# Listed rows turned by VectorE in 32 by 32 blocks, counts from two products, the last block added half by half: one AdaLN block with a mixture of experts on Trainium2

## The chip, the cores and the metric

The kernel runs on one core of a Trainium2 chip. The metric is the device time of one execution in microseconds. Nine runs of the kernel before have a median of 868.95 us (864.46 to 876.58).

## What is computed

One transformer block over `x` of 8 sequences by 512 tokens by 256 features, all in float32. The first half is a layer norm with a modulation, a causal linear attention of 16 heads and an output projection, added to `x`. The second half is a layer norm with a modulation and a mixture of 8 experts. Its core, from the reference:

```
probs = jax.nn.softmax(xf @ router_w.T, axis=-1)
topv, topi = jax.lax.top_k(probs, 2)
topv = topv / (topv.sum(axis=-1, keepdims=True) + 1e-09)
cw = (jax.nn.one_hot(topi, e, dtype=xf.dtype) * topv[..., None]).sum(axis=1)
h = jax.nn.gelu(jnp.einsum('td,edh->teh', xf, w1), approximate=False)
y = jnp.einsum('teh,ehd->ted', h, w2)
out = jnp.einsum('te,ted->td', cw, y)
```

`w1` is 8 by 256 by 1024 and `w2` 8 by 1024 by 256: 1 MB each for one expert. The kernel computes only the two experts that a token is routed to.

## The kernel before, in words

**Routing.** The eight sequences are worked on one after the other, in chunks of 128 tokens. `rows_of` makes one row of 521 floats for each token (256 normed features, the token's number, 8 weights, 256 gate values). `route` (L884) ranks the 8 experts for each token and counts, for each token and expert, how many tokens came before it. That count comes from products into the PSUM tile `at_ps` (L918 to L930): one with the strictly triangular matrix `earlier`, and one with `ones` for each of the four chunks, over all later chunks. With the count, POOL scatters each row twice into the DRAM array `slots` (L963), which has a list for each expert.

**Blocks.** Full units of a list are taken as soon as they are there (`plan`), the rest at the end (`plan_rest`). A block is a pair (256 rows) or a single (128 rows) of one expert. By `TAKE` (L34) there are 9 singles and 10 pairs during the sequences; 17 pairs and 4 singles follow from `plan_rest`, and four more singles stand in a branch at the end that is taken only if a list needs it. That makes 27 pairs and 13 singles outside the branch.

**One block.** `fetch` (L1206) has SP load the expert's `w1` (L1216), its `w2` (L1221) and the rows (L1227, tile `r`), in this order, three buffers of each; which expert and which rows is read from SBUF into a register first. `turn_rows` (L1241) turns the rows: PE transposes of 128 by 128 into PSUM (`x_ps`, L1253), an ACT copy to SBUF (`xT`, L1255). Then `experts` (L1342) alternates first products (`h_ps`, from `w1` and `xT`), ACT's gelu (`g`) and second products (`y_ps`, in `second`, L1282). `finish` (L1295) multiplies `y_ps` by weight and gate on DVE into `y`, and POOL adds each half of 128 rows to the sums with an indirect DMA (L1321): to `acc` in DRAM, and for the last five blocks to the output itself, once `acc` has been copied there (L1306).

**Order.** Nothing is issued as the code is read. All work goes into a plan (`Plan`), which simulates the engines with written-in durations and then issues each engine's instructions in the order found. On each engine this order is fixed: PE waits at a product whose weights are late, and SP waits at a load whose buffer isn't free, with all later loads behind it. A buffer of `w1` becomes free with the last first product of the block three before; one of `w2` with its last second product.

All engine instructions go through a helper and so show line L220; tile names tell them apart.

Of the kernel before, what the change touches and what calls it, by code (L numbers as in the profile page):

```python
# [19 lines left out]
HEADS = 16  # L20
HD = 16
HALF = HD // 2
PAIR = 2 * HD
GH = P // HD
LN_EPS = 1e-5
# [313 lines left out]
def kernel(  # L339
# [57 lines left out]

    SYNC = mybir.DependencyInfo(mybir.DependencyClass.Sync, mybir.DependencyReason.DATA)
    scattered = []
    gathered = []  # L400
    added = []
    copied = []
# [481 lines left out]
    def route(q):  # L884
# [30 lines left out]
        is_in = small([P, NC, E], "is_in")  # L915
        first = small([P, NC, 2, E], "first")
        dve(V.tensor_single_scalar, is_in, rank, 2.0, op=ALU.is_lt)
        at_ps = early_bank(f"at_ps_{b}")  # L918
        with L.group("PE", 1.05):
            product(  # L920
                at_ps[:, : NC * E], earlier, is_in.rearrange("p c e -> p (c e)"),
                start=True, stop=False, skip_group_check=True,
            )
            for c in range(NC):

                product(
                    at_ps[:, (c + 1) * E : (NC + 1) * E].rearrange("p (c e) -> p c e", e=E),
                    ones, is_in[:, c, :].unsqueeze(1).to_broadcast([P, NC - c, E]),
                    start=False, stop=(c == NC - 1), skip_group_check=True,
                )  # L930
        dve(V.tensor_reduce, red, pr, us=0.18, axis=AX.X, op=ALU.add)
        dve(V.tensor_scalar_add, red, red, 1e-9 * LARGE)
        dve(V.reciprocal, red, red)
# [23 lines left out]
        dve(V.tensor_reduce, where, first, us=0.21, axis=AX.X, op=ALU.add)  # L957
        dve(V.tensor_copy, slot, where)
        dve(V.tensor_add, count, count, at_ps[:, NC * E : (NC + 1) * E])
        q.scatters = []  # L960

        def scatter(c, j):
            s = nc.gpsimd.indirect_dma_start(  # L963
                out=slots, out_offset=IndirectOffsetOnAxis(ap=slot.now()[:, c, j : j + 1], axis=0),
                in_=row.now()[:, c, :], in_offset=None,
                bounds_check=NONE - 1, oob_is_err=False,
            )
            apart(s, scattered + cleared, "a slot is of one pair of token and expert")
            apart(s, gathered, "blocks that are read are full by then")
            scattered.append(s)  # L970

        L.level += LEVEL["scatter"]
        for c in range(NC):
            for j in range(2):
                q.scatters.append(
                    L.do(
                        "POOL", 1.29, lambda c=c, j=j: scatter(c, j), r=[slot, row], landing=2.0,
                        mb=0.27,
                    )
                )  # L980
                q.scatters[-1].indirect = True


    def spans(small, n, tag):
# [221 lines left out]
    def fetch(block):  # L1206
        n, nt = block.n, block.nt
        L.level = TOP
        w1_sb = L.tile(wpool, [P, KD, H], "w1", f"w1_{n}", 3)
        w2_sb = L.tile(wpool, [P, NH, D], "w2", f"w2_{n}", 3)  # L1210
        r = L.tile(pb, [P, 2, ROW], "r", f"r_{n}", 3)
        reg = {}

        def weights1():
            reg["e"] = nc.sync.value_load(block.expert_i.now(), min_val=0, max_val=E - 1)
            nc.sync.dma_start(  # L1216
                out=w1_sb.now(), in_=w1[ds(reg["e"], 1)].rearrange("o (k p) h -> p (o k) h", p=P)
            )

        def weights2():  # L1220
            nc.sync.dma_start(  # L1221
                out=w2_sb.now(), in_=w2[ds(reg["e"], 1)].rearrange("o (n p) d -> p (o n) d", p=P)
            )

        def rows():
            at = nc.sync.value_load(block.slot.now(), min_val=0, max_val=NONE)
            got = nc.sync.dma_start(  # L1227
                out=r.now()[:, :nt, :],
                in_=slots[ds(at, nt * P), :].rearrange("(t p) w -> p t w", p=P),
            )  # L1230
            needed = [g for w in block.seen for g in w.given]
            behind(got, needed, "the rows of a block come before it")
            apart(got, [s for s in scattered if s not in needed], "those are of later blocks")
            gathered.append(got)

        L.do("SP", 0.6, weights1, r=[block.expert_i], w=[w1_sb], landing=2.0, mb=1.0)
        L.do("SP", 0.4, weights2, r=[block.expert_i], w=[w2_sb], landing=2.0, mb=1.0)
        L.do("SP", 0.6, rows, r=[block.slot], w=[r], after=block.seen, landing=2.0, mb=0.26 * nt)
        return block, w1_sb, w2_sb, r

    def turn_rows(fetched):  # L1241

        block, w1_sb, w2_sb, r = fetched
        n, nt = block.n, block.nt
        L.level = 1000 + X.k - 1.5
        rest = block.held is not None
        x_ps = late_bank(f"x_ps_{n}") if rest else early_bank(f"x_ps_{n}")
        w = nt * P
        xT = L.tile(pb, [P, KD, 2 * P], "xT", f"xT_{n}", 2)
        with L.group("PE", 0.11 * 2 * nt, hold=[xT]):  # L1250
            for k in range(KD):
                for t in range(nt):
                    turn(x_ps[:, k * w + t * P : k * w + (t + 1) * P], r[:, t, ts(k, P)])  # L1253
        L.level = TOP
        copy(xT[:, :, :w], x_ps[:, : KD * w].rearrange("p (k s) -> p k s", k=KD))  # L1255
        cw = L.tile(pb, [P, 2, 1], "cw", f"cw_{n}", 3)
        cwe = L.tile(pb, [P, 2, E], "cwe", f"cwe_{n}", 3)
        dve(
            V.tensor_mul, cwe[:, :nt], r[:, :nt, CW:GATE],
            block.is_of.unsqueeze(1).to_broadcast([P, nt, E]),  # L1260
        )
        dve(V.tensor_reduce, cw[:, :nt], cwe[:, :nt], us=0.17, axis=AX.X, op=ALU.add)
        to = L.tile(pb, [P, 2], "to", f"to_{n}", 3, I32)
        dve(V.tensor_copy, to[:, :nt], r[:, :nt, TID].bitcast(I32))
        if rest:

            empty = L.tile(pb, [P, 2], "empty", f"empty_{n}", 3, I32)
            instead = L.tile(pb, [P, 2], "instead", f"instead_{n}", 3, I32)
            dve(
                V.tensor_tensor, empty[:, :nt], block.held[:, block.i, :].to_broadcast([P, nt]),  # L1270
                place[:, :nt], op=ALU.is_le,
            )
            fits = block.at_end and nt == 2
            dve(V.tensor_copy, instead[:, :nt], (place if fits else beyond)[:, :nt])
            L.call(
                "DVE", 0.17,
                lambda o, m, d: V.copy_predicated(out=o, mask=m, data=d),
                to[:, :nt], empty[:, :nt], instead[:, :nt], 
            )
        return block, w1_sb, w2_sb, xT, cw, to, r  # L1280

    def second(y_ps, w2_sb, nt, group, n_groups, each, g, level):  # L1282

        L.level = level
        with L.group("PE", 0.433 * each * nt):
            for t in range(nt):
                for i in range(each):
                    product(
                        y_ps[:, ts(t, D)], g[:, i * nt * P + t * P : i * nt * P + (t + 1) * P],
                        w2_sb[:, each * group + i, :],  # L1290
                        start=(group == 0 and i == 0 and t == 0),
                        stop=(group == n_groups - 1 and i == each - 1), skip_group_check=True,
                    )

    def finish(block, cw, to, r, y_ps):  # L1295
        n, nt = block.n, block.nt
        L.level = TOP
        y = L.tile(pb, [P, 2, D], "y", f"y_{n}", 2)
        for t in range(nt):
            dve(  # L1300
                V.scalar_tensor_tensor, y[:, t, :].of(t), y_ps[:, ts(t, D)], cw[:, t, :],
                r[:, t, GATE:], us=0.48, op0=ALU.mult, op1=ALU.mult,
            )
        if block.at_end and X.copies is None:
            def give(b):
# [7 lines left out]
            ]  # L1313
        after = X.adds[-2:] + X.stores[-1:] + (X.copies or [])

        def add():
            halves = []
            for t in range(nt):
                if t:
                    nc.gpsimd.memset(between, 0.0)  # L1320
                s = nc.gpsimd.indirect_dma_start(  # L1321
# [4 lines left out]
                    oob_is_err=nt == 2 or not block.at_end,  # L1326
                )
                apart(s, halves, "a token comes to an expert once")
                behind(s, added[-1:], "one addition to a token after the other")
                if block.at_end:  # L1330
                    behind(s, copied, "and after the sums so far")
                halves.append(s)
            added.extend(halves)

        X.adds.append(
            L.do("POOL", 1.85 * nt, add, r=[to, y], after=after, landing=2.0, mb=0.13 * nt)
        )
        X.adds[-1].indirect = True

    X.stores = []  # L1340

# [58 lines left out]
    for b in range(B):  # L1400
# [20 lines left out]
        route(q)  # L1421
        if TAKE[b][0]:
            L.level = 4 * b + 3 + LEVEL["plan"]
            blocks = plan(b, q.scatters)
            experts(blocks)
    L.level = 4 * B
    blocks, others, more_i = plan_rest(q.scatters)

    def all_of(blocks):
        experts(blocks)  # L1430
        second(*X.pending)
        finish(*X.ending)
        X.pending = X.ending = None

    def give_out():
# [66 lines left out]
```

## Time and profile before

| | |
|---|---|
| median of nine runs | 868.95 us |
| the profiled execution, its own time | 870.08 us |
| its span, first to last instruction | 868.4 us |
| PE busy | 808.3 us (93%) |
| PE weight loads busy | 666.7 us (77%) |
| DVE / ACT / POOL busy | 381.1 / 284.1 / 319.5 us |
| moved by DMA | 154.27 MB in 95167 packets |
| share of the 16 DMA engines, SP's queue / POOL's queue | 44.8% / 12.6% |
| mean granted PE clock | 0.968 |

PE is the busiest engine. The span falls in three parts: up to about 425 us attention and routing with the nine singles in between, then a mixture until about 500 us, then expert blocks alone. "Busy" is time in which an instruction of the engine ran; the idle time of an engine that isn't the bottleneck costs nothing. A "packet" is one contiguous piece that one of the 16 DMA engines moves.

### The profile page before, as it was taken

The page shows a single profiled execution, that of the slowest core. Times are in us where ns is not written, and L with a number is a line of the kernel's source. Part 1 is how long each engine was busy: PE and PEld are TensorE (multiplying, and loading weights), DVE is VectorE, ACT ScalarE, POOL GpSimd, SP SyncE. Part 2 cuts the span into 40 slices and gives each one's busy share as a digit, 9 for nine tenths or more (in the row PEclk, how much of TensorE's full clock was granted, in tenths as well). Part 3 has the DMA queues.
Part 4 walks back from the last instruction along what each step waited for, and adds up shares of the span by engine and source line. Part 5 has one row for each costly group of instructions (what it writes and reads, how often), then busy time and mean ns, then how long its engine had stood idle before and what let it go on. Part 6 is the DMA issues. An engine that isn't in the chain of part 4 may idle for free. (4 is left out here: it accounts for less than half of the span.)

```text
span 868.4 us, 15967 instructions
## 1 busy us (share of the span) xinstructions
PE 808.3 (93%) x5998; PEld 666.7 (77%) x5998; DVE 381.1 (44%) x1290; ACT 284.1 (33%) x617; POOL 319.5 (37%) x477
## 2 busy tenths in 40 slices
PE   5899886998979979899999899999999999999995
PEld 3566665766857867678888688888898989889885
DVE  4889776588777848767527010111111111111000
ACT  3555342443625536354222112222122221222120
POOL 5733544426463453543515612212122112212122
PEclk9999988899999989999999899999999999999999
DMA  7412343853535252624957967667686867858942
GB/s 221 122 29 68 98 151 138 297 140 117 161 131 159 79 186 88 217 70 153 286 181 232 279 189 213 218 185 225 168 258 228 247 177 236 263 176 259 348 89 26
DMA packets 95167, 154.27 MB, mean 178 GB/s; under 512 B 6632, under 2 KB 69736, under 8 KB 94960
## 3 DMA queue, kind: packets, MB, share of 16 engines
q1 hardware_dynamic: 79680, 125.22, 44.8%
q0 software_dynamic: 15408, 28.00, 12.6%
q8 instruction: 49, 0.80, 0.4%
q14 instruction: 30, 0.25, 0.1%
HBM read 120.19 MB, written 37.20 MB: 181 GB/s over the span
## 5 line engine op out<-in xcount | busy, mean ns | idle before, releaser
L220 PE MATMUL y_ps<-w,g 128*128 128x256 f32 x1072 | 257.4, 383 | 7.0 <-issue 7.0
L220 PE MATMUL h_ps<-xT,w 128*128 128x256 f32 (+1 forms) x1280 | 258.2, 352 | 0.2 <-PE x_ps L220 0.2
L220 PEld LDWEIGHTS h_ps<-xT,w 128*128 128x128 f32 x1280 | 217.6, 196 | 24.2 <-issue 0.6
L220 PEld LDWEIGHTS y_ps<-w,g 128*128 128x128 f32 x1072 | 201.4, 192 | 35.0 <-issue 9.3
L1321 POOL DMA_INDIRECT acc<-y,to x57 | 90.1, 1580 | 253.2 <-DVE y L220 205.4
L220 ACT ACTIVATE g<-h_ps 128x512 f32<-128x512 f32 x134 | 80.0, 597 | 313.2 <-PE h_ps L220 299.6
L220 DVE SCALAR_TENSOR_TENSOR y<-y_ps,cw,r 128x256 f32<-128x256 f32 x67 | 29.9, 479 | 165.4 <-PE y_ps L220 156.3
L220 DVE TENSOR_TENSOR sm<-s_ps,causal 128x512 f32<-128x512 f32 x128 | 82.4, 681 | 20.8 <-PE s_ps L220 14.5
L963 POOL DMA_INDIRECT slots<-row,slot x64 | 64.6, 1010 | 37.0 <-issue 13.1
L220 PE MATMUL qk_ps<-wqkv_sb,hT 128*128 128x512 f32 x128 | 64.6, 628 | 1.9 <-ACT hT L220 1.8
L220 POOL TENSOR_TENSOR f<-f,t 128x512 f32<-128x512 f32 x32 | 43.0, 1345 | 54.4 <-DVE t L220 43.2
L220 DVE TENSOR_TENSOR cwe<-r,is_of_rest 128x16 f32<-128x16 f32 (+1 forms) x21 | 3.6, 174 | 130.9 <-DMA r<-slots 122.5
L220 PE MATMUL a_ps<-wo,oT 128*128 128x256 f32 x128 | 37.2, 417 | 16.2 <-ACT oT L220 10.1
L220 PEld LDWEIGHTS s_ps<-qT,kT 32*128 32x128 f32 x1024 | 34.3, 190 | 13.9 <-issue 9.6
L220 PE MATMUL s_ps<-qT,kT 32*128 32x128 f32 x1024 | 41.9, 289 | 2.8 <-ACT kv L220 1.1
L220 PEld LDWEIGHTS a_ps<-wo,oT 128*128 128x128 f32 x128 | 24.4, 203 | 24.5 <-ACT oT L220 13.4
L220 POOL TENSOR_SCALAR mv_f<-mv_f 128x1 f32<-128x1 f32 x32 | 9.9, 309 | 86.7 <-DVE mv_f L220 72.3
L220 PEld LDWEIGHTS qk_ps<-wqkv_sb,hT 128*128 128x128 f32 x128 | 23.8, 201 | 21.0 <-issue 15.2
L220 PE MATMUL v_ps<-wqkv_sb,hT 128*128 128x256 f32 x128 | 37.2, 412 | 2.9 <-ACT hT L220 1.4
L220 PE MATMUL oT_ps<-sm,vz 128*32 128x128 f32 x1024 | 37.2, 281 | 1.8 <-DVE sm L220 1.7
L1321 POOL DMA_INDIRECT out_dram<-y,to x10 | 15.6, 1559 | 52.5 <-DMA out_dram<-acc 22.7
L220 DVE TENSOR_TENSOR x<-x,a_ps 128x256 f32<-128x256 f32 x32 | 13.4, 417 | 48.6 <-PE a_ps L220 45.8
(227 smaller groups left out, 1018.6 us busy)
## 6 DMA issues: line engine op xcount, KB each, us to landing
w<-in_w_dram SPq DMA_DIRECT2D x80, 1024.0 KB, 6.0
r<-slots SPq DMA_DIRECT2D x27, 521.0 KB, 6.1
row<-modd SPq DMA_DIRECT2D x8, 512.0 KB
acc<-x SPq DMA_DIRECT2D x8, 512.0 KB, 2.9
out_dram<-acc SPq DMA_DIRECT2D x8, 512.0 KB, 5.5
x<-in_x_dram SPq DMA_DIRECT2D x7, 512.0 KB, 4.0
r<-slots SPq DMA_DIRECT2D x13, 260.5 KB, 9.6
mod<-modd SPq DMA_DIRECT2D x8, 384.0 KB, 4.5
```

Source lines behind the costliest of these rows:

```text
L220: return method(now(out), *[now(a) for a in args], **{k: now(a) for k, a in kw.items()})
L963: s = nc.gpsimd.indirect_dma_start(out=slots, out_offset=IndirectOffsetOnAxis(ap=slot.now()[:, c, j : j + 1], axis=0), in_=row.now()[:, c, ...
L1321: s = nc.gpsimd.indirect_dma_start(out=out.rearrange("b s d -> (b s) d") if block.at_end else acc, out_offset=IndirectOffsetOnAxis(ap=to.n ...
```

## The change

Four things.

1. **The turning.** The rows' 256 features are no longer loaded with the rest of the row. Four DMAs load them into a new tile `sx`, in which partition 32q + p holds, for each group of 32 rows, the 64 features from 64q on of row p of the group. One DVE transpose, which turns each 32 by 32 block in place, makes `xT` from it. The PE transposes, `x_ps` and the ACT copy go. The rest of the row (265 floats) stays in `r`, loaded by a fifth DMA.
2. **w1 in another order.** In `xT` the features now stand as (q, k, c) with k between q and c, so the rows of `w1` have to stand so too: partition 32q + c of part k holds row 64q + 32k + c. `w1` is loaded by two DMAs, one for each k. On the DRAM side such a DMA walks 4 groups (q) of 32 rows (c) of 1024 floats; on the SBUF side 128 partitions.
3. **The counts.** DVE sums `is_in` over the chunks into `up_to` (four small operations), and one product with `ones` takes the place of four.
4. **The last block.** Its second products, its multiplication and its additions are recorded for each half by itself.

`turn_rows` also moves from the level of its block to the top level of the plan, and a block now names all scatters so far instead of its own sequence's.

```
-        with L.group("PE", 1.05):
+        up_to = small([P, NC, E], "up_to")
+        dve(V.tensor_single_scalar, up_to, rank, 2.0, op=ALU.is_lt)
+        for c in range(1, NC):
+            dve(V.tensor_add, up_to[:, c, :], up_to[:, c - 1, :], up_to[:, c, :])
...
+        with L.group("PE", 0.45):
...
-            for c in range(NC):
-
-                product(
-                    at_ps[:, (c + 1) * E : (NC + 1) * E].rearrange("p (c e) -> p c e", e=E),
-                    ones, is_in[:, c, :].unsqueeze(1).to_broadcast([P, NC - c, E]),
-                    start=False, stop=(c == NC - 1), skip_group_check=True,
-                )
+
+            product(
+                at_ps[:, E : (NC + 1) * E], ones, up_to.rearrange("p c e -> p (c e)"),
+                start=False, stop=True, skip_group_check=True,
+            )
...
-        r = L.tile(pb, [P, 2, ROW], "r", f"r_{n}", 3)
+        sx = L.tile(pb, [P, 8, KD, Q], "sx", f"sx_{n}", 3)
+        r = L.tile(pb, [P, 2, ROW - D], "r", f"r_{n}", 3)
...
-            nc.sync.dma_start(
-                out=w1_sb.now(), in_=w1[ds(reg["e"], 1)].rearrange("o (k p) h -> p (o k) h", p=P)
-            )
+            parts = w1[ds(reg["e"], 1)].rearrange("o (q k c) h -> k (o q) c h", k=KD, c=Q)
+            for k in range(KD):
+                nc.sync.dma_start(out=w1_sb.now()[:, k, :], in_=parts[k])
...
-            got = nc.sync.dma_start(
-                out=r.now()[:, :nt, :],
-                in_=slots[ds(at, nt * P), :].rearrange("(t p) w -> p t w", p=P),
-            )
+            rows_ = slots[ds(at, nt * P), :]
...
+            parts = [
+                (
+                    sx.now()[q * Q : (q + 1) * Q, : 4 * nt].rearrange("p t k c -> p t (k c)"),
+                    rows_[:, q * KD * Q : (q + 1) * KD * Q].rearrange("(t p) c -> p t c", p=Q),
+                )
+                for q in range(P // Q)
+            ]
+            parts.append((r.now()[:, :nt, :], rows_[:, D:].rearrange("(t p) w -> p t w", p=P)))
+            for out_, in_ in parts:
+                got = nc.sync.dma_start(out=out_, in_=in_)
...
-        L.do("SP", 0.6, rows, r=[block.slot], w=[r], after=block.seen, landing=2.0, mb=0.26 * nt)
+        L.do("SP", 1.0, rows, r=[block.slot], w=[sx, r], after=block.seen, landing=2.0, mb=0.35 * nt)
...
-        with L.group("PE", 0.11 * 2 * nt, hold=[xT]):
-            for k in range(KD):
-                for t in range(nt):
-                    turn(x_ps[:, k * w + t * P : k * w + (t + 1) * P], r[:, t, ts(k, P)])
-        L.level = TOP
-        copy(xT[:, :, :w], x_ps[:, : KD * w].rearrange("p (k s) -> p k s", k=KD))
+        dve(
+            V.transpose, xT[:, :, : nt * P].rearrange("p k (t c) -> p k t c", c=Q),
+            sx[:, : 4 * nt].rearrange("p t k c -> p k t c"),
+        )
...
-        with L.group("PE", 0.433 * each * nt):
-            for t in range(nt):
-                for i in range(each):
...
+        for halves in [[t] for t in range(nt)] if apart_ else [range(nt)]:
+            with L.group("PE", 0.433 * each * len(halves)):
+                for t in halves:
+                    for i in range(each):
...
-        second(*X.pending)
-        finish(*X.ending)
+        second(*X.pending, apart_=True)
+        finish(*X.ending, apart_=True)
```

## The prediction

> **What bounds the kernel now.** I read first the busy times by stretch (all engines, PE clock, DMA share), to see which limit holds where.
>
> ```profile
> core 0: us, PE busy (x) PEld busy (x) DVE busy (x) ACT busy (x) POOL busy (x), PEclk, DMA share, GB/s
> ...
> 425.00:500.00 75.00, 70.73 (x423) 61.39 (x422) 27.89 (x129) 17.37 (x33) 31.81 (x52) 0.95 0.75 238
> 500.00:800.00 300.00, 300.00 (x1495) 265.78 (x1494) 37.77 (x169) 62.44 (x108) 67.06 (x84) 1.00 0.71 217
> 800.00:868.00 68.00, 59.66 (x283) 52.19 (x281) 5.46 (x18) 11.42 (x20) 15.91 (x19) 0.97 0.56 160
> ```
>
> From 500 to 800 us PE has no gap: 300.00 of 300 us, at full clock. The 16 DMA engines are busy for 0.71 of it, so loads have 29% to spare, as a mean over sixteen engines. The sequencer's waits of SP say why the loads are not late:
>
> ```profile
> SPq L1216 <- PE h_ps L220: 243.4, 34, 25.8
> SPq L1221 <- PE y_ps L220: 98.4, 26, 6.3
> ```
>
> (us in total, times, longest.) SP stands waiting for PE to free a buffer of `w1` (243.4 us) or `w2` (98.4 us); PE waits for no load of a block anywhere in its list of waits. Last the timeline of one block:
>
> ```profile
> 601.18 0.60 PE L220 MATMUL x_ps<-ident,r 128*128 128x128 f32 x4
> ...
> 601.62 1.89 PE L220 MATMUL y_ps<-w,g 128*128 128x256 f32 x8
> 601.82 0.58 ACT L220 COPY xT<-x_ps 128x512 f32<-128x512 f32 x1 [1.51 <-PE x_ps L220]
> ...
> 603.35 3.62 PE L220 MATMUL h_ps<-xT,w 128*128 128x256 f32 x16
> ```
>
> (start, us, engine.) Four transposes hold PE from 601.18 to 601.62: 0.44 us for a pair. `w1` is issued at 585.39, 599.65 and 613.90, so a pair takes 14.25 us of PE; 627.93 to 635.40 gives 7.47 us for a single.
>
> **The change, part by part: what it removes.** Turning: 27 pairs at 0.44 us and 13 singles at 0.22 (615.43 to 615.65) are 14.7 us of PE. Its ACT copies (20.6 us) were hidden; they are nothing. Counts: the products into `at_ps` take 10.46 us in 80 records, 0.13 each; six of ten per sequence go: 8 x 6 x 0.13 = 6.3 us, in a stretch where PE is some 90% busy; I count 5. For that DVE gets four small operations per sequence (0.15 to 0.18 us in rows of that size, such as `is_in`, 0.174): 0.7 us on the way to the scatter, covered by POOL's and PE's other work; 5 us if nowhere covered. The last block: its second half's multiply ends at 860.58 and the two adds run at 860.46 and 862.32. With the halves apart the first add starts some 1.7 us earlier (eight records, 1.73 us), the second right after its own multiply: 1.4 us. In all 21 us, if the blocks' loads keep up. A pair would then take 13.8 us, a single 7.25.
>
> **What it adds on DVE and SP.** One transpose per block. No DVE transpose is in the trace; the nearest rows, DVE operations of 128x512, take 0.68 to 0.82 us and 128x256 0.42 to 0.57. I take 0.7 and 0.45; from nothing to twice that it stays hidden, since DVE is busy 37.77 of 300 us there, and the rows land well before they are needed (issue 604.86, first use on DVE 610.49, on PE 615.43). In the built order the transpose sometimes stands ahead of the multiply of an earlier block, which frees the one `y_ps` bank; that matters only if rows are late. SP issues eight DMAs for a block, not three, at 0.2 to 0.4 us each (0.37 for `w`, 0.21 to 0.26 for `r`): some 3 us of 13.8, hidden.
>
> **What it adds on the DMA engines.** Here prices of one packet are needed: share x 16 x width / packets. The first fence is a stretch with `w1` alone (560 to 561 us), the second with `w2` alone (576 to 577), the third the start with small rows (7 to 8), the fourth POOL's queue from 570 to 780.
>
> ```profile
> DMA packets 104, 0.43 MB, mean 426 GB/s; under 512 B 0, under 2 KB 0, under 8 KB 104
> ...
> q1 hardware_dynamic: 104, 0.43, 103.3%
> ```
>
> ```profile
> DMA packets 235, 0.24 MB, mean 241 GB/s; under 512 B 0, under 2 KB 235, under 8 KB 235
> ...
> q1 hardware_dynamic: 235, 0.24, 79.2%
> ```
>
> ```profile
> DMA packets 930, 0.30 MB, mean 304 GB/s; under 512 B 673, under 2 KB 930, under 8 KB 930
> ...
> q1 hardware_dynamic: 930, 0.30, 125.9%
> ```
>
> ```profile
> q0 software_dynamic: 4176, 3.80, 11.7%
> ```
>
> That is 159 ns for 4 KB, 54 for 1 KB, 22 as a mean over mostly small ones, and 94 for an added row with its closing packets. A piece of `sx` has 256 B: between 22 and 54; I take 22, as 673 of those 930 are smaller still than 512 B. On all 16 engines a pair then costs each engine 16 x 159 (`w1`) + 64 x 54 (`w2`) + 64 x 22 (`sx`) + 16 x 54 (the rest of the row) + 18 x 94 (adds) = 2.5 + 3.4 + 1.4 + 0.9 + 1.7 = 9.9 us, 12.0 with 54 for `sx`. Both are under 13.8: small pieces alone bind nothing.
>
> The decisive question is on how many engines a half of `w1` runs. Its DRAM side now has an outermost loop of 4 (q) and not of 128 rows, because k lies between q and c. In the trace every load but one has 128 or 16 outermost. The exception is the store `modd<-modr` of 8 rows of 4 KB, alone in 26.9 to 28.6 us:
>
> ```profile
> DMA packets 16, 0.03 MB, mean 19 GB/s; under 512 B 8, under 2 KB 8, under 8 KB 16
> ```
>
> Eight data packets and eight small ones that close them. Over the whole run the page has 6632 packets under 512 B. Take off the 1536 rows of the four loads with rows of 32 and 64 B, and 16 for each of POOL's 139 indirect DMAs: 2872 are left, which is 179 x 16 + 8, and SP issued 180 DMAs. So a closing packet comes once per engine, sixteen ordinarily, eight where eight was outermost. The trace has no case with different counts on the two sides, here 4 and 128. The two ends are 16 engines (9.9 us, hidden) and 4. The nearest row is the 8-row store, where the small outermost count set the engines; I take 4.
>
> The Trainium skill, page "DMA: Bandwidth & Descriptors", section "Why a DMA increments its semaphore by 16 and not by 1", speaks against the change in the same place: it says the largest number up to 16 is taken that divides the slowest dimension of both sides, always the lowest-numbered engines. By it both halves would go to the same four engines, and the sum would be the forecast below; the row of the 8-row store agrees with it (8), and no run here shows the case of 4 against 128.
>
> With four engines each gets 2 x 32 = 64 packets of 4 KB: 64 x 159 = 10.2 us for `w1`, on top of its share of the rest (3.4 + 1.4 + 0.9 + 1.7 = 7.4): 17.6 us for a pair; 10.2 + 3.4 + 0.7 + 0.4 + 0.9 = 15.6 for a single. The smaller prices were read beside sixteen busy engines, and here twelve are often idle, so I take a little less: 17.0 and 15.2. PE needs 13.8 and 7.25. **The loads of a block become the bound.** Three buffers hide this only for a while; the nine singles, which come 15 us or more apart and are mostly loaded far ahead, lose nothing.
>
> The sum, by the chain of loads. Before, the thirteenth block's `w1` (the fourth pair) is issued at 446.99 us, and from there issues come every 14 to 17 us, so from then on the four engines have a load waiting at all times. Left to load are 24 pairs and 4 singles: 24 x 17.0 + 4 x 15.2 = 469 us. On the same engines run the last sequence's eight scatters and eight zeroings after 462 us, 16 x 8 rows per engine at 94 ns, 12 us, of which I count 10; and the copies of `acc` to the output, 8 x 512 KB, at the page's best slice of 348 GB/s 12 us. The earlier part is 6 us shorter (counts and the singles' turns). 447 - 6 + 469 + 10 + 12 = 932 us for the last block's rows. In the trace of before the last block's first product starts at 840.50 and the span ends at 868.4: 27.9 us, less 1.4 for the halves: 26.5. 932 + 26.5 = 958.5 of span; the profiled execution's time is 1.7 us over its span (870.08 against 868.4), so 960 us. That execution lies 0.1% above the median of 868.95, so no correction.
>
> **Rivals.**
> (A) *Sixteen engines after all*: the transfer is spread over the 128 SBUF rows, the loads stay hidden and PE stays the bound: 870 - 21 = **849 us**, faster. For it: everything else in the sum is a gain; against it: the 8-row store. It decides by count: a pair's load is 256 x 159 / n + 7.4 us on n engines, under 13.8 from n = 6.4 on; with 8 engines A holds too.
> (B) *Four engines, but other four for each half*: 32 packets, 5.1 + 7.4 = 12.5 us, under 13.8; singles at 10.5 pass PE's 7.25, but three pairs and a single need 48 against 48.7. Just hidden, **855 us**. Nothing in the profile speaks for it.
> (C) *Small pieces as dear as 1 KB on top of four engines*: `sx` 64 x 54 = 3.4, pair 19.6, single 16.6: 447 - 6 + 537 + 22 + 28 = **1028 us**.
>
> That the changed kernel does not do what it says gets none of the chance: the built order has no transposes of rows on PE and one on DVE per block.
>
> **How the numbers follow.** Forecast 0.77, A 0.12, B 0.04, C 0.07. The forecast's own spread: with 15.5 and 13.8 (every price a tenth lower) and no scatter in the way 447 - 6 + 427 + 12 + 28 = 908; to C above. The range 900 to 1025 leaves A, B and half of C out. A measurement of this kernel can tell about 0.5% from no change: faster 0.16, same 0.01, slower 0.83.
>
> **What would show it.** Right: PE waits for `w` or `xT` in the last 400 us and is busy some 80% of them; SP's waits for `h_ps` shrink, or turn into few; the mean DMA share falls to about 0.6 though loads are late; a `w1` half takes 5 us or more and closes with 4 small packets. Wrong: PE full from 500 us on and pairs every 13.8 us means A or B; pairs every 19 us or more means C. PE records of `at_ps` should fall from 80 to 32, and `x_ps` be gone, in every case.

## The result and the profile after

The changed kernel takes 1061.42 us (median of 20 runs, 1055.06 to 1068.13) against 870.33 us for the kernel before: 1.219 times as long (95% interval 1.217 to 1.221). The forecast was 960 us with a range up to 1025. The direction and the mechanism were right, the size forecast was half of what it is: 90 us forecast, 191 measured. All later runs are compared with runs of the kernel before in the same series, which take 820 to 823 us there and 870 in the last one (`multiply_first`): in the profile of before at 870 ACT and DVE stand still for 59.2 us without a releaser that it can name, in one at 822 (`before_here`) they don't; in the changed kernel it is 79.5 us at 1061 and nothing at 1016 (`after_here`). What these waits are is not shown.

The stretches of the changed kernel that answer to those shown of before (same columns):

```profile
425.00:500.00 75.00, 65.98 (x611) 53.78 (x612) 39.40 (x129) 24.53 (x57) 30.55 (x50) 0.91 0.44 136
500.00:800.00 300.00, 236.10 (x1102) 202.48 (x1101) 53.72 (x231) 40.87 (x71) 67.26 (x96) 0.90 0.65 163
800.00:1060.00 260.00, 184.73 (x812) 158.23 (x810) 26.67 (x103) 28.66 (x48) 41.05 (x51) 0.86 0.59 146
```

Where PE had no gap it now stands still for a fifth of the time, at a granted clock of 0.90 and not 1.00. No engine takes its place, and the DMA share fell from 0.71 to 0.65: the loads are late while the sixteen engines are, on the mean, less busy than before. DVE waits 285.0 us for the rows that it turns, and SP's waits for PE say that the loads are no longer early:

```profile
DVE xT L221 <- DMA sx<-slots: 285.0, 23, 17.2
```

```profile
SPq L1230 <- PE y_ps L221: 44.2, 8, 12.7
...
SPq L1227 <- PE h_ps L221: 17.0, 3, 16.5
```

SP waited 243.4 us for PE to free a `w1`; now it waits 17.0. What holds SP instead is seen in its own timeline, two blocks of it (start, length, what is issued):

```profile
742.20 11.77 SPq L1247 DMA_DIRECT2D sx<-slots  x4
754.21 0.86 SPq L1247 DMA_DIRECT2D r<-slots  x1
755.92 1.56 SPq L1227 DMA_DIRECT2D w<-in_w_dram  x2
758.18 0.39 SPq L1230 DMA_DIRECT2D w<-in_w_dram  x1
759.92 11.56 SPq L1247 DMA_DIRECT2D sx<-slots  x4
771.73 0.36 SPq L1247 DMA_DIRECT2D r<-slots  x1
772.94 1.42 SPq L1227 DMA_DIRECT2D w<-in_w_dram  x2
```

Four DMAs of 64 KB take 11.56 us to issue, right behind a `w1` and a `w2`; 10.01 us of them are the issue of the second alone. In the same stretch of before a DMA takes 0.2 to 0.4 us. So SP is held, once for each block. Nothing in the trace names what ends the hold; I read it as SP waiting for room in the queues of the engines under `w1`, which would then have a backlog nearly all the time. The next `w1` comes 17 us later.

That a half of `w1` runs on four engines is counted on the page:

```profile
DMA packets 131716, 154.30 MB, mean 146 GB/s; under 512 B 43176, under 2 KB 114856, under 8 KB 131504
```

Of the 43176 small packets 34304 are pieces of `sx` (27 x 1024 + 13 x 512), 1536 rows of small tables and 2224 the closing packets ("closers") of POOL's 139 DMAs. 5112 are left for SP's 380 DMAs: 299 x 16 + 8 + 80 x 4. Each of the 80 halves closes four times.

That it is the same four engines for both halves, and that they are behind, is seen in the landings of `w2`, which runs on sixteen. Of the sixteen closers of the `w2` issued at 758.18 us, twelve land 6.9 to 7.5 us after the issue and four 16.8 to 18.6 us after it. In each of the last 22 blocks it is twelve within 8 us and four after 14 to 20. From 748 to 753 us, between the two groups, 4.07 packets are under way on the mean (from the start and length of the trace's packet records).

### The profile page after: what moved, and what is told of

Read it like the earlier page. It is cut to its first block, busy times and chain, and to the rows that moved or that the text cites. A ratio compares the mean times of both kernels' runs of the same rounds, so it can differ in the third digit from the quotient of the medians.

```text
span 1059.6 us, 16287 instructions
## 1 busy us (share of the span) xinstructions
PE 837.7 (79%) x5816; PEld 676.9 (64%) x5816; DVE 403.3 (38%) x1362; ACT 272.0 (26%) x583; POOL 316.9 (30%) x475
## 2 busy tenths in 40 slices
DMA packets 131716, 154.30 MB, mean 146 GB/s; under 512 B 43176, under 2 KB 114856, under 8 KB 131504
## 5 line engine op out<-in xcount | busy, mean ns | idle before, releaser
L221 PE MATMUL y_ps<-w,g 128*128 128x256 f32 x1072 | 280.7, 409 | 120.2 <-issue 116.9
L221 PEld LDWEIGHTS y_ps<-w,g 128*128 128x128 f32 x1072 | 216.4, 206 | 159.5 <-issue 123.7
L221 PE MATMUL h_ps<-xT,w 128*128 128x256 f32 (+1 forms) x1280 | 266.5, 357 | 8.6 <-issue 8.6
L221 PEld LDWEIGHTS h_ps<-xT,w 128*128 128x128 f32 x1280 | 222.6, 199 | 38.4 <-issue 11.0
L221 DVE STREAM_TRANSPOSE xT<-sx 128x512 f32<-128x512 f32 (+1 forms) x40 | 24.9, 624 | 349.5 <-DMA sx<-slots 285.0
L221 PE MATMUL qk_ps<-wqkv_sb,hT 128*128 128x512 f32 x128 | 70.8, 681 | 1.6 <-ACT hT L221 1.0
L221 PE MATMUL s_ps<-qT,kT 32*128 32x128 f32 x1024 | 49.7, 304 | 21.1 <-issue 13.4
L221 PEld LDWEIGHTS s_ps<-qT,kT 32*128 32x128 f32 x1024 | 39.9, 201 | 35.2 <-issue 24.2
L221 PE MATMUL v_ps<-wqkv_sb,hT 128*128 128x256 f32 x128 | 40.6, 443 | 3.2 <-ACT hT L221 2.1
L1337 POOL DMA_INDIRECT out_dram<-y,to x10 | 15.6, 1555 | 84.4 <-DMA sx<-slots 48.6
L221 PE MATMUL cum_ps<-f,causal 128*128 128x256 f32 x64 | 22.5, 432 | 20.0 <-DVE f L221 18.8
```

The lines of the kernel that those rows point to most:

```text
L221: return method(now(out), *[now(a) for a in args], **{k: now(a) for k, a in kw.items()})
L1337: s = nc.gpsimd.indirect_dma_start(out=out.rearrange("b s d -> (b s) d") if block.at_end else acc, out_offset=IndirectOffsetOnAxis(ap=to.n ...
```

## The experiments

Times and ratios are medians; intervals are 95%.

### How many engines: `before_4`, `before_8`, `before_16`, `halves_128`

The kernel before, where only the load of `w1` is changed (c = 32, 16 and 8 give 4, 8 and 16 groups):

```
-  out=w1_sb.now(), in_=w1[ds(reg["e"], 1)].rearrange("o (k p) h -> p (o k) h", p=P)
+  parts = w1[ds(reg["e"], 1)].rearrange("o (q k c) h -> k (o q) c h", k=KD, c=32)
+  for k in range(KD):
+      nc.sync.dma_start(out=w1_sb.now()[:, k, :], in_=parts[k])
```

> The kernel before with `w1` loaded in two halves whose DRAM side walks 4 groups of 32 rows, as in the changed kernel; nothing else is changed (PE turns the rows, `r` is one DMA). The rows of `w1` then stand in another order than the features that they are multiplied with, so the output is another. If four engines are the cause: 1020 to 1060 us, a little less than the changed kernel, as the 256 B pieces (64 x 21 ns = 1.3 us for a pair on each engine) are not there. If small pieces, the number of DMAs or DVE are the cause: under 900 us.

> As the kernel before with two halves of `w1`, but each walks 8 groups of 16 rows (output another, for the same reason). If the engines follow the outermost count, each of eight gets 32 packets of 4 KB for a block: 32 x 159 to 199 ns = 5.1 to 6.4 us, and with its share of the rest (6.0 to 7.5 us for a pair, without `sx`) 11 to 14 us against PE's 14.25 for a pair and 9 to 10 against 7.47 for a single: about hidden, 868 to 890 us. If it were the loss of order or the splitting of `w1` that costs, it would stand near the one with 4 groups.

> The same with 16 groups of 8 rows (output another): sixteen engines. If engines are the cause: 870 us, as the kernel before (866 to 875). If splitting `w1` into two DMAs or walking it with a gap costs by itself: above 880.

> The kernel before with `w1` in two DMAs of 128 rows each (k = 0 and 1), in the kernel before's own order. It tells what made a 4 KB packet take 268 ns with 16 groups of 8 rows, against 185: if it is the splitting in two, it is 250 ns or more here too; if it is how the rows are dealt to the sixteen engines, it is 180 to 190 ns. The time is that of the kernel before in both cases (ratio 0.997 to 1.007), as PE still has no gap.

Measured: 1.265 (1.257 to 1.272), 1.098 (1.091 to 1.104), 1.007 (1.004 to 1.010) and, with 128 rows in each half, 1.001 (0.999 to 1.004). The stretch from 500 to 780 us of `before_4`, then of `before_16`, then of `halves_128`:

```profile
500.00:780.00 280.00, 225.75 (x1002) 193.30 (x1001) 22.18 (x99) 42.28 (x72) 60.66 (x84) 0.90 0.65 162
```

```profile
500.00:780.00 280.00, 279.84 (x1395) 247.56 (x1394) 34.70 (x155) 57.57 (x99) 60.32 (x76) 1.00 0.86 227
```

```profile
500.00:780.00 280.00, 280.00 (x1398) 248.55 (x1397) 34.83 (x155) 57.47 (x99) 59.63 (x75) 1.00 0.73 229
```

The first has all the signs of the changed kernel, PE at 81% and the DMA share at 0.65, without `sx`, without a DVE transpose and with four DMAs for a block. The small packets on the pages are 6312, 6632 and 7272 for 4, 8 and 16 groups: each step of four engines adds 80 x 4 = 320, each of eight 640. So the outermost count of the DRAM side sets the engines, and small pieces and the eight DMAs for a block are not the cause. The run with eight goes against the condition of a rival: eight engines are not hidden, they cost 80 us. A 4 KB packet took 243 ns there (mean of the trace's packet records from 500 to 780 us), 32 of them 7.8 us.

The last two stretches have the same bytes on sixteen engines and differ in DMA share, 0.86 against 0.73: with 16 groups of 8 rows a 4 KB packet takes 268 ns, with 128 rows 175. Splitting `w1` in two costs nothing that shows (1.001); walking its rows in 16 groups makes the packets longer, and the kernel by some 0.6% (1.007 against 1.001).

### The changed kernel on sixteen engines: `w1_by_q`, `w1_one_dma`, `rows_in_order`

```
   (w1_by_q)
+  parts = w1[ds(reg["e"], 1)].rearrange("o (q k c) h -> q c (o k) h", k=KD, c=Q)
+  for q in range(P // Q):
+      nc.sync.dma_start(out=w1_sb.now()[q * Q : (q + 1) * Q], in_=parts[q])
   (w1_one_dma: the load of the kernel before)
   (rows_in_order: as w1_one_dma, and)
+  for k in range(KD):
+      dve(V.scalar_tensor_tensor, row.rearrange("p (q k c) -> p k q c", k=KD, c=Q)[:, k],
+          scaled[:, ts(k, P)].rearrange("p (q c) -> p q c", c=Q), mv[:, 0, 1:2], ...)
```

> The changed kernel with one edit: `w1` is loaded by four DMAs, one for each q (32 partitions, both k), so that the outermost loop is 32 rows on both sides; a block has ten DMAs, not eight. If the number of DMA engines under `w1` sets the time (four engines), all of the loss goes: about 850 us (846 to 858), PE full from 500 us on. If the 256 B pieces of `sx` and the five row DMAs set it, or the number of DMAs in flight, the time stays above 1000 us, and with ten DMAs for a block it could become longer than 1061.

> The changed kernel with `w1` loaded by one DMA as in the kernel before (128 partitions, rows k*128 + p), so seven DMAs for a block, with `sx` and its transpose kept; the rows of `w1` then stand in another order than the features, so the output is another. With `w1` by q the loss was gone but the gain of 21 us did not show (ratio 1.0037), and the 4 KB packets took 293 ns (159 in the kernel before's own profile), the DMA share was 0.97. If it is this layout of `w1` (32 partitions at a time) that eats the gain, here it shows: ratio 0.975 to 0.985, 4 KB packets near 185 ns. If the small pieces of `sx` or the wait for them eat it, the ratio stays at 1.00.

> A version with the right output: the features are written into the rows in the order (q, k, c) by DVE (two multiply-adds of 128 features for one of 256, 32 operations more), the router's weights are loaded in that order, and `w1` stays as in the kernel before, in one DMA. The rest is the changed kernel. Ratio 0.975 to 0.99 if the layout of `w1` ate the gain; it should stand 0 to 8 us above the one before, by 32 operations of 0.25 us on DVE in a stretch where DVE is 75% busy. 1.00 or more if the gain is lost elsewhere.

Measured: 1.0037 (1.0002 to 1.0071), 0.9894 (0.9875 to 0.9913) and 0.9857 (0.9835 to 0.9879). With ten DMAs for a block and all of `sx` the loss is gone, which settles the cause. But `w1_by_q` gains nothing. Its stretch, and that of `rows_in_order`:

```profile
500.00:780.00 280.00, 276.41 (x1339) 243.71 (x1338) 46.92 (x180) 47.18 (x80) 58.39 (x74) 1.00 0.97 233
```

```profile
500.00:780.00 280.00, 279.59 (x1358) 247.55 (x1357) 47.76 (x183) 49.02 (x82) 62.86 (x80) 1.00 0.81 233
```

The same 233 GB/s fill the engines to 0.97 in the one and to 0.81 in the other. The 4 KB packets take 293 ns where a DMA writes 32 partitions and 183 ns where it writes 128. `rows_in_order` puts the features into the rows in the order that the transpose needs, so that `w1` needs no new order at all. A pair takes 13.81 us there (`w1` issued at 506.75, 520.57, 534.38, 548.19), where 13.8 was forecast for sixteen engines. It is 1.4% faster than the kernel before.

### Where the loss is made: `after_here`, `late_four`, `early_four`

```
             if block.held is None:      # late_four; "is not None" for early_four
+                (the four DMAs of w1_by_q)
             else:
                 (the two halves)
```

> The changed kernel itself on the same chip as the others. In the profile on which the prediction was made, ACT and DVE stand still for 59 us without a releaser that the profile can name, and the kernel before takes 870 us; on the chips of the later runs it takes 820 to 823 us and no such wait is there. If those waits only add to either kernel, the changed kernel takes 1035 to 1050 us here, a little over the kernel before with `w1` on four engines (1035.5); the difference to that one bounds what eight DMAs for a block and 256 B pieces cost. Under 1000 us, the waits would be part of the loss.

> The changed kernel, where the 19 blocks that are taken while the sequences run load `w1` by four DMAs, one for each q (sixteen engines), and the 21 blocks at the end keep the two halves on four engines. If the loss is the pace of the last blocks alone: in the changed kernel the 20th block's `w1` is issued at 584.6 us and the end comes 431 us later; in the kernel before it is issued at 509 us. 509 + 431 = 940 us (925 to 950). If the four engines cost nothing while the sequences run, as the prediction had it, it stays at 1000 us or more.

> The other way round: halves on four engines for the 19 blocks that are taken while the sequences run, four DMAs by q for the 21 at the end. If the early blocks cost what the issue times say (584.6 against 509 us at the 20th block): 820 + 70 = 890 us (875 to 900). If the early blocks lose nothing, as the prediction had it for the singles, and only the pairs among them lose by the pace (10 x 3 to 4 us): 855 to 865 us.

Measured: the changed kernel 1015.78 us (1.2345, 1.2295 to 1.2396), four engines at the end only 942.2 us (1.1475), while the sequences run only 900.7 us (1.0982). `late_four` came out inside its expectation and `early_four` at the upper edge of its. `after_here` came out 20 us under its own; it is below `before_4`, which still turns rows on PE, so the small pieces cost nothing that shows. Over `w1_by_q` the two halves of the loss are 118 and 78 us (0.1438 and 0.0945 of 820), together 196, against 189 for the changed kernel: they add up. By the prediction's own terms the 21 blocks at the end lose 98 us (17 pairs by 3.2 us, 4 singles by 7.95, output copies 12) and everything before them 32 (7 pairs by 3.2, scatters 10). So the late part was 20 us short, and the early part 45. The division is rough: these terms add up to 130 and the forecast lay only 111 over its own 849 for sixteen engines.

Within the early part, the profiles of `early_four` and `w1_by_q` differ by 30 us at the issue of the 13th `w1` (431.7 against 401.4) and by 41 more at that of the 20th (584.1 against 513.2). The first holds the nine singles and three pairs, the second seven pairs.

The early part in SP's timeline of `after_here`, from 145 to 193 us:

```profile
150.99 12.84 SPq L1227 DMA_DIRECT2D w<-in_w_dram  x2
164.02 1.92 SPq L1230 DMA_DIRECT2D w<-in_w_dram  x1
166.99 12.66 SPq L1227 DMA_DIRECT2D w<-in_w_dram  x2
179.90 1.84 SPq L1230 DMA_DIRECT2D w<-in_w_dram  x1
181.84 10.37 SPq L1445 DMA_DIRECT2D acc<-x  x1
192.31 1.73 SPq L657 DMA_DIRECT2D mod<-modd  x1
```

and the same place of `before_here`:

```profile
148.74 4.27 SPq L1216 DMA_DIRECT2D w<-in_w_dram  x1
153.25 0.55 SPq L1221 DMA_DIRECT2D w<-in_w_dram  x1
164.38 0.37 SPq L1414 DMA_DIRECT2D acc<-x  x1
165.06 0.37 SPq L853 DMA_DIRECT2D row<-modd  x1
166.89 4.87 SPq L1227 DMA_DIRECT2D r<-slots  x3
171.86 1.13 SPq L655 DMA_DIRECT2D mod<-modd  x1
```

The singles do come in bursts: three blocks' weights in a row. The second and the third `w1` hold SP for 12.84 and 12.66 us, where the third of `before_here` holds it for 4.27, and `mod`, which belongs to the attention, is issued at 192.31 and not at 171.86. Two waits of `after_here` follow from it (100 to 300 us: total, times, longest):

```profile
DVE wo L221 <- DMA mod<-modd: 23.3, 2, 19.6
...
PE cum_ps L221 <- DVE f L221: 18.0, 1, 18.0
```

### Is it that wait by itself? `mod_by_act`

```
-            "SP", 0.4,
-            lambda: nc.sync.dma_start(
+            "ACT", 0.4,
+            lambda: nc.scalar.dma_start(
                 out=q.mod.now().rearrange("p n d -> p (n d)"),
```

> The changed kernel with one edit: the load of `mod` for each sequence is issued by ACT and not by SP, so it no longer stands behind the halves of `w1`. If SP held at issuing is a loss by itself (PE stands 18.0 us for `mod` at about 190 us), the time falls from 1015.8 to 995 to 1000 us. If the loads on the four engines set when the 13th block can begin, whatever PE does meanwhile, it stays at 1010 to 1018 us, and the wait moves to the rows or the weights of a block.

Measured: 1041.4 us (1.2675, 1.258 to 1.277). The wait for `mod` fell to 3.3 us, and the time went up. Two waits from 100 to 430 us:

```profile
PE qk_ps L221 <- ACT hT L221: 22.8, 2, 21.9
ACT hT L221 <- DMA sx<-slots: 22.4, 1, 22.4
```

The edit moved the wait to ACT and did not take it away. From 177.5 to 200.0 us ACT's sequencer stands at the issue of `mod` until a load that SP had issued lands; `mod` goes out at 200.10, and the `hT` behind it, for which PE waits, starts at 200.47. So the run does not tell whether this wait is a loss by itself, and which load costs how much of the 78 us is not separated.

### What sets the pace: `no_w2_late`

```
+        if block.held is None:
+            X.w2_sb = L.tile(wpool, [P, NH, D], "w2", f"w2_{n}", 3)
+        w2_sb = X.w2_sb
```

> The changed kernel without the loads of `w2` for the 21 blocks at the end (they use the last `w2` that was loaded; the output is another). On the four engines a block then has `w1` (64 x 4 KB), `sx`, the rest of the rows and the additions. If the 4 KB packets take 200 ns because `w2` runs on the same engines, they fall to 160 to 175 ns and the pace from 18.2 to about 14 us: 1016 - 21 x 4 = 930 us. If their price belongs to the four engines (all four writing 32 neighbouring partitions each), it stays near 200 ns, and only w2's own packets go (64 x 72 ns = 4.6 us, of which part ran beside `w1`): 15 us or more, 945 us and above.

Measured: 932.3 us (1.136). The `w1` issues of this kernel, 13.8 us apart where the changed kernel has 18.2:

```profile
666.59 1.41 SPq L1229 DMA_DIRECT2D w<-in_w_dram  x2
680.35 1.41 SPq L1229 DMA_DIRECT2D w<-in_w_dram  x2
694.16 1.40 SPq L1229 DMA_DIRECT2D w<-in_w_dram  x2
```

The 4 KB packets fell from 201 to 177 ns (means of the late stretch), not quite to the 160 to 175 that I named: somewhat more than half of what a packet took over the 159 ns of a `w1` alone came from `w2` on the same engines. The pace by itself tells less. From the 20th to the 38th block it is 13.9 us on the mean, and the packets of `w2` alone, 64 x 71 ns = 4.5 us, would also take 18.2 to 13.7. PE's own 13.8 us for a pair and singles of 7.25 would give 12.6 on the mean, so loads still bind, by little; SP again waits 32.3 us for PE to free a `w1` between 600 and 860 us.

### The order on DVE: `multiply_first`

In the changed kernel PE's longest waits are named "y_ps <- issue" (116.9 us, 16 times), not a load. What stands behind them is read from the timeline of the profiled run, around one of them:

```profile
748.12 0.60 ACT L221 ACTIVATE g<-h_ps 128x512 f32<-128x512 f32 x1 [2.86 <-PE h_ps L221]
...
759.34 0.71 DVE L221 STREAM_TRANSPOSE xT<-sx 128x512 f32<-128x512 f32 x1 [15.78 <-DMA sx<-slots]
...
759.97 0.83 DVE L221 SCALAR_TENSOR_TENSOR y<-y_ps,cw,r 128x256 f32<-128x256 f32 x2
...
760.91 3.65 PE L221 MATMUL y_ps<-w,g 128*128 128x256 f32 x8 [12.88 <-issue]
```

A transpose waits 15.78 us for its rows, and behind it on DVE stands the multiplication of an earlier block that empties the one `y_ps` bank. PE has second products to do and can't.

```
+        turned.behind |= set(X.muls)   # the transpose behind the last multiplication
```

> The changed kernel with one edit in the plan: the transpose of a block comes on DVE behind the multiplication of the block two before, which frees the `y_ps` bank. In the changed kernel PE stands 116.9 us (16 times) before `y_ps`, because the transpose ahead of that multiplication waits for `sx`. If that order costs by itself, the pace falls and the time from 1015.8 by up to 16 x 3.5 = 56 us (the second products that PE could do meanwhile), to 960 us. If the four engines set the pace, PE's waits only move from `y_ps` to `h_ps`, and the ratio stays within 1 to 2% of 1.2345.

Measured: 1.2277 (1.2214 to 1.234), as slow as the changed kernel (1.219 in the series of the result, 1.2345 in another). But the edit did not do what it was to do:

```profile
764.08 0.18 DVE L221 TENSOR_TENSOR cwe<-r,is_of_rest 128x16 f32<-128x16 f32 x1 [16.55 <-DMA r<-slots]
...
764.65 0.87 DVE L221 SCALAR_TENSOR_TENSOR y<-y_ps,cw,r 128x256 f32<-128x256 f32 x2
...
765.62 3.68 PE L221 MATMUL y_ps<-w,g 128*128 128x256 f32 x8 [12.74 <-issue]
```

The block's weights (`cwe`), which need the same rows, now stand ahead of the multiplication, and PE waits as before (126.7 us). Whether the order on DVE costs anything beside the loads in the run of blocks is therefore open; SP's hold in every block speaks for the loads. At the end of the changed kernel, where no later load can hide it, it does cost:

```profile
1026.12 5.89 PE L221 MATMUL y_ps<-w,g 128*128 128x256 f32 x16 [15.57 <-issue]
1031.84 1.89 PE L221 MATMUL h_ps<-xT,w 128*128 128x256 f32 x8
```

The last block's rows are turned at 1024.12 us. The multiplication that empties `y_ps` stands behind that on DVE, so sixteen second products of the block before, whose gelu had ended at 1011.24, run only from 1026.12, and the last block's first product starts at 1031.84, some 7 us after its rows are there.

### The small parts: `counts_alone`, `five_products`, `own_bank`, `best_mix`

`counts_alone` is the kernel before with the diff's part on `up_to`; `five_products` is `rows_in_order` without it. `own_bank` adds to `five_products`:

```
+            last = rest and nt == 2 and not (X.todo or X.fetched or X.turned)
+            y_ps = [y_ps, early_bank(f"y2_ps_{n}") if last else y_ps]
```

`best_mix` is `rows_in_order` with that bank. `before_here` is the kernel before.

> The kernel before with the counts from two products alone. The prediction had 5 us for it: ratio 0.994. Where PE waits for others at that place, the 6.3 us of products were no part of the path: ratio 0.998 to 1.002.

> The kernel before itself, for a profile from the same chip as the others: PE full from 500 us on, and the 4 KB and 1 KB packets' prices to compare with those of the others.

> The version with the rows written in order (ratio 0.9857), with the counts as in the kernel before (five products). If the new counts lose 3.4 us as alone (ratio 1.0041), this one gains them: ratio 0.981 to 0.984. If the loss of the counts alone was a shift of the planned order that only that kernel has: 0.986 to 0.99.

> As the version with five products, with the second half of the last block's second products in a PSUM bank of its own. In the changed kernel the first half's multiplication waits for all sixteen records of PE on the one bank, and the halves gain nothing. If the shared bank is the reason, the multiplication of the first half now starts some 1.7 us before PE ends, and the first addition as much earlier; the end comes 0.5 to 1.7 us earlier against the version with five products (ratio lower by 0.001 to 0.002, at the edge of what can be told). If something else holds it, the trace stays as it was.

> The version with the rows in order and the new counts (ratio 0.9857), with the second half of the last block in a PSUM bank of its own. If the bank gives the 0.9 us that the trace of that run shows, ratio 0.983 to 0.986; it would be the fastest of all versions.

Measured: `counts_alone` 1.0041 (1.0025 to 1.0057), `five_products` 0.9973 (0.9953 to 0.9993), `own_bank` 0.9949 (0.9928 to 0.9971), `best_mix` 0.9868 (0.9835 to 0.9902). The counts take 5.3 us of products off PE (`at_ps` 9.68 us before, 4.43 after) and yet cost 3.4 us alone; beside the transposes on DVE they gain 9.5 us (0.9857 against 0.9973), and 6.6 with the bank. Neither branch of my expectation of `five_products` came true. I take it that the plan puts out another order each time and that an effect of 5 us drowns in that; this is not shown, and which part of the order does it I did not find.

The bank does part of what was asked. The end of the changed kernel, and that of `own_bank`:

```profile
1047.38 3.62 PE L221 MATMUL y_ps<-w,g 128*128 128x256 f32 x16
...
1051.04 0.88 DVE L221 SCALAR_TENSOR_TENSOR y<-y_ps,cw,r 128x256 f32<-128x256 f32 x2 [11.21 <-PE y_ps L221]
1051.80 1.55 POOL L1337 DMA_INDIRECT out_dram<-y,to  x1 [8.64 <-DVE y L221]
```

```profile
804.50 3.62 PE L221 MATMUL y_ps<-w,g 128*128 128x256 f32 x16
...
807.30 0.48 DVE L221 SCALAR_TENSOR_TENSOR y<-y_ps,cw,r 128x256 f32<-128x256 f32 x1 [10.35 <-PE y_ps L221]
808.06 1.55 POOL L1344 DMA_INDIRECT out_dram<-y,to  x1 [7.77 <-DVE y L221]
```

In the first both multiplications start when PE's sixteen products are done, the addition 4.42 us after these began. In the second the first half starts 0.82 us before PE ends (1.7 expected), and the addition comes 3.56 us after they began. The gain of 0.9 us is at the edge of what the times can tell; `best_mix` is no faster than `rows_in_order`.

## Why the prediction was right, and where it was wrong

**Right: four engines.** The step from the 8-row store to the half of `w1` held, to the packet. The Trainium skill, page "DMA: Bandwidth & Descriptors", section "Why a DMA increments its semaphore by 16 and not by 1", has the same rule (the largest number up to 16 that divides the slowest dimension of both sides); the closers of the 4, 8 and 16 groups now show it for 4 against 128 too. Rival B, other four engines for each half, is out by the landings of `w2`, four late and not eight; its load, 32 packets of `w1` on each of eight engines, is that of `before_8` (900.7 us). Of the signs named these were there: SP's waits for `h_ps` shrink (17.0 us), the DMA share is 0.64 from 600 to 1000 us though loads are late, and PE is busy 75% there (80% named). That PE waits for `w` or `xT` was not seen by name: its longest waits stand before `y_ps`, and it is DVE that waits for the rows.

**Wrong: "the nine singles ... lose nothing".** This step put a term at nothing. The thirteenth block's `w1` is issued at 474.3 us and not at 441, a third of what is missing. The singles do not come "15 us or more apart": in the trace of before the second, third and fourth `w1` are issued at 149.56, 153.20 and 159.34 us, and on SP's queue the attention's own loads stand behind them. I did not read the order of the blocks on the queue. `early_four` puts 78 us on all 19 early blocks, 30 of them in the stretch with the singles.

**Too small: the pace.** 17.0 us for a pair and 15.2 for a single, 16.7 on the mean, were 18.2. 64 packets was right, their price was not. 159 ns and 54 ns were read where one load ran alone; in the changed kernel they are 200 and 71 ns, a piece of the rest of the row 61 and not 54, a packet of the adds 103 and not 94. Taken together that is 21.5 us for a pair, more than the 18.2 that pairs and singles take. So a sum of packet times overstates, and the two errors partly cancelled, which is luck. That packets overlap shows in the prediction's third fence: a share of 125.9% of sixteen engines is more than sixteen packets one after the other can give. "A little less" was the wrong way to lean. In before's own late stretch the mean of the 4 KB packets was already 184 ns, and that was there to be used.

The 101 us of span that were missing (1059.6 against 958.5), along the forecast's chain:

| step | forecast | measured | off |
|---|---|---|---|
| issue of the 13th `w1` | 441 | 474.3 | +33 |
| 13th to 18th block (5 pairs and the scatters) | 95 | 117.1 | +22 |
| 18th to 39th block (17 pairs, 4 singles; 21 x 18.2) | 350 | 382.2 | +32 |
| 39th block to the end (2 blocks, copies, last block) | 72.5 | 86.0 | +14 |

The second row is 26 us over five blocks at the late pace (117.1 less 5 x 18.2), where 10 were counted for scatters and zeroings; what they take of it is not separated. Inside the last the copies of `acc` take about 9 and not 12 (1000.5 less 973.6 less 18.2). The rest of it is the last block: from the issue of its `w1` to its turned rows 23.6 us where 17 were taken, from there to its first product 7.7 where nothing was (the second products held on DVE), and to the end 27.8 where 26.5 were.

**Wrong: with eight engines "A holds too".** It cost 9.8%. At the prices of that run a pair sums to 15.6 us on an engine (32 x 243 ns for `w1`, 64 x 71 for `w2`, 16 x 100 for the rows, 18 x 93 for the adds), more than PE's 14.25, though such sums overstate. PE waits 31.0 us for rows there, but SP still waits 215.3 us for PE to free a `w1`, so not every block is late, and how the 80 us come together is not shown. **Right: the small pieces.** A 256 B piece took 21 ns (22 taken, 54 in rival C); that the time lies nearer to C's 1028 than to the forecast has other reasons. **Right: the transpose**, 0.71 and 0.45 us, and hidden whenever rows are early. That its place on DVE matters "only if rows are late" was right too, and they were.

**The gains.** Of 21 us, 9 to 12 are there on sixteen engines (0.9894, 0.9857). The turning taken off PE is real after 500 us: 13.81 us for a pair, and 8 us less from the 20th `w1` to the end (303.4 against 311.4, `rows_in_order` against `before_here`). Up to the 20th `w1` only 2.3 us are gained (506.75 against 509.06), and with the counts left as they were the whole kernel gains 2.2 (0.9973). So the counts were no term to count on, and the gains do not add up term by term. The halves gave nothing: the step "the first add starts some 1.7 us earlier" took the two halves of one PSUM bank for two things that are waited for apart, and in this kernel they are not.

**The range** went from prices a tenth lower to the dear small pieces of C, all by the block. It had no case in which the 4 KB packets themselves are dearer, and none in which loads of the stage before are late as well.

## What to carry to other kernels

Before a load is rearranged, look at the outermost dimension of both sides: here a transfer whose outer count was 4 ran on four DMA engines, and the mean DMA share went down (0.71 to 0.65) while the load got late. Take packet prices from the busiest stretch that the trace has, and look which other loads stand behind the slower one on its queue, in the stage before too. Where a layout needs another order of features, it can be cheaper to write the activations in that order once (0.9857 here) than to fetch the weights so for every block (1.0037 on sixteen engines).

## What the runs showed of the hardware that was not expected

- The same bytes on sixteen engines at other prices. A 4 KB packet of `w1` took 175 to 186 ns when a DMA walks 128 rows to 128 partitions, 268 ns as 16 groups of 8 rows, and 293 ns when each DMA fills 32 partitions; the DMA share went from 0.73 to 0.86 and, with `sx`, 0.97. Why is not shown; all three have sixteen closers.
- SP is held while it issues, 10 to 13 us for DMAs of 64 to 512 KB that in before mostly take 0.2 to 0.4 us, when a transfer on four engines is ahead. With sixteen engines it happens too, seldom and shorter (4.27 us for a third `w1` in a row in `before_here`). No wait in the lists shows it; it is seen only in the length of the issue.
- A load that is late can show as a wait for nothing. PE's 116.9 us before `y_ps` carry the word "issue"; in the one followed above, the load waited for stands behind DVE, ahead of the multiplication on its queue.
